# Folding W_self with W_c1 in the list stage of a two-layer graph kernel, with three orders of work changed beside it

## The chip, the cores and the metric

The kernel runs on one core of one Trainium2 chip. The metric is the device time of one execution in microseconds, as a median of runs. The core has five engines that run their own instruction streams in order: TensorE (PE, matmuls and their weight loads), VectorE (DVE), ScalarE (ACT), GpSimd (POOL) and SyncE (SP). SP issues most of the plain transfers, POOL issues the indirect ones, and ACT issues a few. They wait for each other by semaphores.

## The reference, cut to what matters

Two graph layers over 4096 nodes with 512 features, each with a residual and a layer norm. The adjacency matrix adj (4096 x 4096, int32) has about four ones in a row.

```python
# layer 0: graph attention, 8 heads of 64
Wh = einsum('nf,hfo->hno', x, W)
e  = leaky_relu(f1[:, :, None] + f2[:, None, :], 0.2)      # f1, f2 = Wh . a
attn = softmax(where(adj > 0, e, NEG_INF))
x = layernorm(x + concat_heads(attn @ Wh))
# layer 1: mean over neighbours
agg = (adj > 0) @ x / max(deg, 1)
out = concat([x @ W_self + b_self, agg @ W_nb + b_nb]) @ W_comb + b_comb
x = layernorm(x + relu(out))
```

With W_comb split into an upper half W_c1 and a lower half W_c2, layer 1 is x (W_self W_c1) + agg (W_nb W_c2) + one bias row, which is b_self W_c1 + b_nb W_c2 + b_comb. The kernel multiplies the weights first and calls that a fold.

## The kernel before, in words

Nodes are taken in 32 blocks of 128. All matmuls named here are float32 and fill 128 x 128 of the array. The order of the instructions on every engine is written out by hand: the program text is the order, and a tile name with its number of buffers says what may be reused when. PSUM tiles go by bank names: `tp` (1 buffer), `key` (1), `pw`, `nm` and `sm` (2 each).

**List stage.** It turns each row of adj into a short list of neighbours and computes Wh. The loop runs over b = 0 to 28. Step b loads adj of block b+2 in two halves of 1024 KB (tile `at`, 4 buffers, L389), loads a block of x, transposes x of block w+1 (`transposed`, L320, into `tp`, copied to `xT` by ACT), masks adj of block b+1 on ACT (L395, tile `ab`, 3 buffers), and calls `node_block`: half 0 of Wh (L341, into `pw`, copied by DVE to `row`, L345), the product that packs the masks of block b into keys (`fold_adj`, L413, into `key` or `nm`), the maxima of the keys on DVE (L428), half 1 of Wh, and the store of the row of Wh to the table t0 in HBM (L905, issued by POOL). In steps 6 and 13 two blocks of Wh are made. Every fourth step starts `decode`, which spreads the making of lists for four blocks over the next steps, mostly on DVE. In steps 22, 23 and 24 a further block is transposed only to be summed (`only=True`): DVE reduces it from PSUM (L330). Blocks 29 to 31 of adj follow the loop.

**Layer 1 of the schedule (reference layer 0)** is a loop over i = -2 to 32 with a pipeline over blocks. POOL gathers five groups of 128 rows of t0 for a block (`gather`, L590, 5 buffers of blocks). PE forms sums of weights (`a_shared_sum`, L638), spreads them back (`a_reach`, L657) and forms the shared products (`a_shared`, L684). DVE weighs and adds (L672, L694, L696) and forms the moments (L700); ACT normalises (L707 to L716). PE transposes the normalised block (L320) and multiplies it with the folded W_nb W_c2 (`a_z`, L721), and the row goes to the table t1. In steps 2 to 5 DVE adds b_nb's part to `brow` (`fold_bias`, L300); in step 7 SP loads W_self and W_c1; in steps 16 to 19 DVE adds b_self's part; in step 20 a matmul with ones sums `brow` over partitions (L308, copied by ACT, L309).

**Layer 2 (reference layer 1)** gathers five groups of rows of t1 for a block with 7 buffers of blocks, six late groups (`gather_late`, tile `gl`) among them. For a block PE forms the product with the folded W_self W_c1 (`g_self`, L753) and the shared products (`g_shared`, L760); ACT puts the bias row (L744) and the first gathered row (L734) in PSUM; DVE adds (L738, L740) and forms the output (L776, L780); ACT normalises; SP stores. Ahead of the first product with `m1`, `fold_weights` runs: for each of four chunks c, `turned` transposes 128 rows of W_self (L269, bank `key`, copied by ACT, L270), and four matmuls with W_c1 (L281, bank `tp`) give rows of the product, which ACT copies over `m1` (L285).

The lines of the loop of layer 1 that the change reorders:

```python
        if on(i):
            XT[i] = transposed(i, wp)
            store_xT(i, XT[i])
        if on(i + 2):
            a_shared_sum(i + 2)
        ...
        if on(i + 1):
            a_shared(i + 1)
```

Of the kernel before, what the change touches and what calls it, by code (L numbers as in the profile page):

```python
# [31 lines left out]
F32 = mybir.dt.float32  # L32
# [8 lines left out]
P = 128  # L41
# [49 lines left out]
def listed_layers(  # L91
# [15 lines left out]
    nc = tc.nc  # L107
    N, FIN = x.shape
    H, _, D = w0.shape
    NB = N // P  # L110
    FB = FIN // P
    HD = H * D
# [138 lines left out]
    def load_fold(k, w, wr, wc):  # L251
        nc.sync.dma_start(wr, w.rearrange("(c p) o -> p c o", p=P))
        nc.sync.dma_start(
            wc, w_comb[k * HD : (k + 1) * HD, :].rearrange("(c p) o -> p c o", p=P)
        )
        return wr, wc
# [6 lines left out]
            )  # L263
        return brw

    def turned(wr, c, wT):
        tp = ps.tile([P, FB, P], F32, name="key", bufs=1)
        for d in range(FB):
            nc.tensor.transpose(tp[:, d, :], wr[:, c, ts(d, P)], ident)  # L269
        nc.scalar.copy(wT, tp.rearrange("p c r -> p (c r)"))  # L270
        return wT.rearrange("p (c r) -> p c r", c=FB)

    def fold_weights(loaded, place):

        wr, wc = loaded
        wT = turned(wr, 0, place(0))
        for c in range(FB):
            nxt = turned(wr, c + 1, place(c + 1)) if c + 1 < FB else None
            mp = ps.tile([P, HD], F32, name="tp", bufs=1)
            for d in range(FB):  # L280
                nc.tensor.matmul(  # L281
                    mp, lhsT=wT[:, d, :], rhs=wc[:, d, :], start=(d == 0), stop=(d == FB - 1)
                )
                if d == FB - 1:
                    nc.scalar.copy(wr[:, c, :], mp)  # L285
                yield
            wT = nxt

    def bias_columns(brw):

# [6 lines left out]
    def fold_bias(loaded, bcol):  # L297

        for d in range(FB):
            nc.vector.scalar_tensor_tensor(  # L300
                brow, loaded[1][:, d, :], bcol[:, d : d + 1], brow, OP.mult, OP.add
            )
            yield
# [11 lines left out]

    def transposed(b, wp, sums=None, only=False):

        tp = ps.tile([P, FB, P], F32, name="tp", bufs=1)
        for c in range(FB):
            nc.tensor.transpose(tp[:, c, :], xs[:, b, ts(c, P)], ident)  # L320
        if only:
            t = tp
        else:
            t = wp.tile([P, FB, P], F32, name="xT", bufs=2)
        if sums is None or b >= EARLY and not only:
            nc.scalar.copy(t, tp)  # L326
        elif only or b % 2 == 0:
            if not only:
                nc.scalar.copy(t, tp)
            nc.vector.tensor_reduce(sums[:, :, b : b + 1], tp, AX.X, OP.add)  # L330
        else:
            for c in range(FB):
                nc.scalar.activation(
                    t[:, c, :], tp[:, c, :], AF.Copy, accum_out=sums[:, c, b : b + 1]
                )
        return t
# [56 lines left out]
    def mask_adj(b, h):  # L393
        ab = masks[b, h] = bp.tile([P, NG // NH, SC], BF16, name="ab", bufs=3)
        nc.scalar.activation(  # L395
            ab, loads.pop((b, h)), AF.Relu, accum_out=asum[:, b, h : h + 1]
        )
# [236 lines left out]
    def a_shared_sum(b):  # L634

        DN[b] = ps.tile([P, H], F32, name="sm", bufs=2)
        for k in range(KH):
            nc.tensor.matmul(  # L638
                DN[b], lhsT=OWN[b][:, k, :], rhs=E[b][:, K0 + k, :],
                start=(k == 0), stop=(k == KH - 1),  # L640
            )
# [40 lines left out]
    def a_shared(b):  # L682
        for k in range(KH):
            nc.tensor.matmul(  # L684
                NM[b], lhsT=OWN[b][:, k, :], rhs=G0[b][:, K0 + k, H:TW],
                start=False, stop=(k == KH - 1), skip_group_check=True,
            )

    def a_adds(b, wp):

        yp = ps.tile([P, HD], F32, name="pw", bufs=2)
        a_weigh(b, slice(0, 1), yp)
        a_weigh(b, slice(1, K0))
        nc.vector.tensor_add(yp, yp, G0[b][:, 1, H:TW])  # L694
        Y[b] = wp.tile([P, HD], F32, name="y", bufs=2)
        nc.vector.tensor_add(Y[b], yp, G0[b][:, 2, H:TW])  # L696
# [106 lines left out]
    def weight(pool, name):  # L803
        return pool.tile([P, FB, HD], F32, name=name)
# [75 lines left out]
    bcol = bias_columns(brw)  # L880


    def node_block(w, xT, between=None):
        row = wp.tile([P, FW], F32, name="row", bufs=2)
        node_half(w, 0, xT, w_sb, row)
        if between is not None:
            fold_adj(between, dp)
            max_keys(between)
        node_half(w, 1, xT, w_sb, row)
        node_rest(w, row)  # L890
        store(w, row, nc.gpsimd)
        return row

    def on_own(b):
# [9 lines left out]
    def store(w, row, eng=nc.scalar):  # L904
        eng.dma_start(t0[2 + w * P : 2 + (w + 1) * P, :], row[:, 0:TW])  # L905

    w, lists = 0, []
    for b in range(LB - 1):
        for k in range(1 + (b in AHEAD)):
            load_x(w + k + XL)  # L910
        load_adj(b + 2, ap)
        if b == 4:
            pads(wp)
        for k in range(2):
            some(lists)
        for k in range(1 + (b in AHEAD)):
            nxt = transposed(w + 1, wp, sums)
            if k == 0 and b in (22, 23, 24):
                transposed(EARLY + b - 22, wp, sums, True)
            if k == 0:  # L920
                key_bank(b + 1)
                for h in range(NH):
                    mask_adj(b + 1, h)
            node_block(w, xT, None if k else b)
            w, xT = w + 1, nxt
        for k in range(2):
            some(lists)
        if b == 16:
            lates = late_lists(dp, fp.tile([P, FB * HD // P, P], F32, name="wr"))
        if b >= 16:  # L930
            next(lates, None)
        if b == 25:
            pieces = mean_row(w_sb, sums, xa)
        if b >= 25:
            next(pieces, None)
        if b % G == G - 1:
            lists = [decode(b + 1 - G, dp, on_own)]
    load_adj(LB + 1, ap)
    node_block(w, xT)
    key_bank(LB)  # L940
    mask_adj(LB, 0)
    m2 = weight(fp, "wr")
    loaded = load_fold(1, w_nb, m2, weight(fc, "wc"))
    fold_adj(LB - 1, dp)
# [45 lines left out]
    def on(b):  # L990
        return 0 <= b < NB
# [3 lines left out]
    for i in range(-2, NB + 1):  # L995
        if on(i):
            a_moments(i)
        if on(i - 1 + GA):
            G0[i - 1 + GA] = gather(t0, i - 1 + GA, gps[(i - 1 + GA) % GA])
        elif i > 0:  # L1000
            b = i - 1 + GA - NB
            G1[b] = gather_early(b, gps[(NB + b) % GA])
        if on(i + 1):
            a_reach(i + 1)
        if i == -1:
            for k in range(2):
                next(m2s)
        if i >= -1 and on(i + 2):
            a_owned(i + 2, wq)
        if on(i + 1):  # L1010
            a_x(i + 1)
            a_normed(i + 1)
            a_weigh(i + 1, slice(K0, KS))
        if on(i + 2):
            a_weights(i + 2, wq)
        if on(i):
            root(i, xs[:, i, :])
        if on(i + 2):
            a_exp(i + 2)
        for k in range({-2: 3}.get(i, 0)):  # L1020
            some(lists)
        if on(i):
            norm(i, xs[:, i, :])
        if on(i - 1):
            a_z(i - 1, XT.pop(i - 1), m2, wp)
        if on(i + 1):
            a_adds(i + 1, wq)
        if on(i):
            XT[i] = transposed(i, wp)
            store_xT(i, XT[i])  # L1030
        if on(i + 2):
            a_shared_sum(i + 2)
            for k in range({-2: 1}.get(i, 0)):
                some(lists)
            a_sum(i + 2, wq)
            for k in range({-2: 1}.get(i, 0)):
                some(lists)
        for k in range({-2: 3, -1: 2}.get(i, 0)):
            next(m2s)
        if on(i + 1):  # L1040
            a_shared(i + 1)
        if on(i + 3):
            a_owners(i + 3, wp)
        if 2 <= i < 6:
            next(biased)
        if i == 7:
            loaded = load_fold(0, w_self, m1, weight(fc, "wc"))
        if 16 <= i < 20:
            if i == 16:
                biased = fold_bias(loaded, bcol[:, 0:FB])  # L1050
            next(biased)
        if i == 20:
            sum_bias()


# [15 lines left out]
    for b in range(2):  # L1071
# [2 lines left out]
        g_shared(b, G1[b])  # L1074
        g_adds(b, G1[b], wq)
        G1[b + GB] = gather(t1, b + GB, gps[b])
    for _ in fold_weights(loaded, place):
        pass
    for b in range(2):
        nxt = load_xT(b + 1, wp)  # L1080
        g_self(b, xT, m1)
# [447 lines left out]
```

## Time and profile before

| what | us |
|---|---|
| median of 3 runs (lowest, highest) | 692.57 (690.92, 694.48) |
| the profiled execution: its time | 690.14 |
| the profiled execution: its span | 688.4 |
| busy PE, DVE, ACT, POOL in the span | 622.5, 499.1, 456.0, 348.8 |
| last mask of adj on ACT starts | 229.18 |
| first gather of t0 starts | 232.54 |
| last product L721 of layer 1 starts | 483.35 |
| first shared product of layer 2 starts | 488.22 |
| last shared product of layer 2 ends | 677.1 |

All durations come from one profiled execution; its time is its span and 1.7 us around it. The list stage lasts to about 232 us, the start of layer 1 overlaps it to about 268, layer 1 lasts to 488 and layer 2 to the end. In the lines of a timeline the first number is the start in the span, the second the duration (of a whole group where instructions are merged, xN), and the bracket the idle time of the engine before it with what ended it. PE's busy time counts matmuls whose ends are modelled, so a busy PE isn't PE at its peak.

### The profile page before, as it was taken

What the parts mean: (1) busy time and instruction counts of PE and PEld (TensorE: products, weight loads), DVE (VectorE), ACT (ScalarE), POOL (GpSimd) and SP (SyncE); (2) the same over time, 40 slices, a digit from 0 to 9 for tenths busy, and PEclk for the clock granted to TensorE, in tenths of its full rate; (3) what the DMA queues carried; (4) which work ended last, traced back from release to release, by engine and by line L of the source; (5) the groups of instructions that cost most, each with busy time, mean ns of one, the idle gap of its engine ahead of it and who ended that gap; (6) DMA issues with size and microseconds to landing.
All of it is one profiled execution on the core that took longest, in us unless ns stands there. A gap on an engine that the chain in (4) does not pass through costs nothing.

```text
span 688.4 us, 9188 instructions
## 1 busy us (share of the span) xinstructions
PE 622.5 (90%) x2354; PEld 344.6 (50%) x2354; DVE 499.1 (72%) x1431; ACT 456.0 (66%) x1044; POOL 348.8 (51%) x411
## 2 busy tenths in 40 slices
PE   4798988987799597999999999999899999999993
PEld 2466766665567354545455445454344444444441
DVE  6237987998598787999998998897304666666663
ACT  3687988878487534767676767776316567767764
POOL 4011111110001477777677776746676677777760
PEclk9989999999899698999999999999999999999997
DMA  8999999999799877989989888868878899998992
GB/s 249 405 408 408 409 408 409 407 409 407 262 321 354 298 193 213 281 277 277 379 275 290 260 275 259 279 209 281 271 210 278 283 297 311 317 308 299 323 306 76
DMA packets 91974, 209.65 MB, mean 305 GB/s; under 512 B 13694, under 2 KB 13702, under 8 KB 91914
## 3 DMA queue, kind: packets, MB, share of 16 engines
q1 hardware_dynamic: 63024, 114.05, 44.8%
q0 software_dynamic: 28704, 94.66, 44.1%
q8 instruction: 21, 0.34, 0.2%
q14 instruction: 39, 0.32, 0.2%
q10 hardware_dynamic: 186, 0.28, 0.1%
HBM read 175.25 MB, written 33.69 MB: 304 GB/s over the span
## 4 chain that ended last, share of the span: by engine, by line
PE 56%; DVE 4%; DMA 4%; POOL 3%; issue 3%; ACT 2%; SPq 0%; DVEq 0%; POOLq 0%; ACTq 0%
PE pw L721 13%; PE nm L753 8%; PE pw L753 8%; PE nm L684 7%; PE nm L760 4%; PE pw L760 4%; POOL g L590 3%; PE tp L281 2%; PE tp L320 2%; PE pw L341 2%; PE sm L657 2%; DMA wc<-in_L_gnn_W_comb_dram 2%; PE sm L638 1%; DMA g<-t,idx 1%; DMA t<-row 1%
## 5 line engine op out<-in xcount | busy, mean ns | idle before, releaser
L590 POOL DMA_INDIRECT g<-t,idx x290 | 280.3, 967 | 109.1 <-issue 49.7
L395 ACT ACTIVATE ab<-at 128x2048 bf16<-128x2048 int32 x64 | 122.3, 1912 | 41.0 <-DMA at<-in_adj_dram 27.8
L341 PE MATMUL pw<-w_sb,xT 128*128 128x264 f32 x512 | 134.4, 409 | 7.0 <-issue 3.8
L721 PE MATMUL pw<-wr,xT 128*128 128x512 f32 x256 | 117.7, 603 | 0.7 <-ACT xT L326 0.7
L341 PEld LDWEIGHTS pw<-w_sb,xT 128*128 128x128 f32 x512 | 97.1, 199 | 36.0 <-issue 7.7
L352 POOL COPY f1s<-lst 128x24 f32<-128x24 f32 x32 | 7.8, 245 | 183.1 <-DVE fmax L349 100.5
L672 DVE TENSOR_TENSOR g<-g,key 128x1024 f32<-128x1024 f32 x64 | 77.9, 1217 | 1.1
L721 PEld LDWEIGHTS pw<-wr,xT 128*128 128x128 f32 x256 | 46.3, 191 | 47.2 <-issue 46.3
L684 PE MATMUL nm<-g,own 128*128 128x512 f32 x128 | 64.5, 627 | 0.0
L320 PE MATMUL tp<-ident,xs 128*128 128x128 f32 x268 | 44.9, 293 | 18.3 <-DVE sums L330 12.1
L753 PE MATMUL pw<-m,xT 128*128 128x512 f32 x128 | 57.6, 592 | 0.0
L753 PE MATMUL nm<-m,xT 128*128 128x512 f32 x128 | 57.6, 592 | 0.0
L320 PEld LDWEIGHTS tp<-ident,xs 128*128 128x128 f32 x268 | 32.3, 150 | 46.7 <-ACT xs L716 21.7
L707 ACT ACTIVATE xs<-y,ln_sum 128x512 f32<-128x512 f32 x32 | 23.1, 723 | 42.2 <-DVE y L700 40.2
L776 DVE SCALAR_TENSOR_TENSOR sm<-y,lst,nm 128x512 f32<-128x512 f32 x16 | 12.1, 756 | 52.9 <-PE nm L770 29.1
L345 DVE COPY row<-pw 128x264 f32<-128x264 f32 x64 | 26.9, 424 | 23.0 <-PE pw L341 17.4
L753 PEld LDWEIGHTS pw<-m,xT 128*128 128x128 f32 x128 | 24.4, 190 | 30.6 <-issue 30.3
L753 PEld LDWEIGHTS nm<-m,xT 128*128 128x128 f32 x128 | 24.4, 190 | 30.6 <-issue 30.6
L590 POOL DMA_INDIRECT g<-t,idxe x30 | 28.4, 947 | 18.2 <-issue 5.5
L281 PE MATMUL tp<-wc,row 128*128 128x512 f32 x64 | 30.9, 622 | 2.0 <-ACT m L285 1.2
L760 PE MATMUL nm<-g,own 128*128 128x512 f32 x64 | 30.2, 594 | 1.2 <-ACT nm L744 1.2
L684 PEld LDWEIGHTS nm<-g,own 128*128 128x128 f32 x128 | 22.5, 196 | 16.3 <-issue 15.6
(210 smaller groups left out, 1068.3 us busy)
## 6 DMA issues: line engine op xcount, KB each, us to landing
at<-in_adj_dram SPq DMA_DIRECT2D x64, 1024.0 KB, 10.7
t<-row POOLq DMA_DIRECT2D x32, 260.0 KB, 5.5
xt<-xT SPq DMA_DIRECT2D x32, 256.0 KB, 4.0
t<-row SPq DMA_DIRECT2D x32, 256.0 KB, 4.2
xT<-xt SPq DMA_DIRECT2D x32, 256.0 KB, 5.4
out_dram<-row SPq DMA_DIRECT2D x32, 256.0 KB, 5.2
xs<-in_x_dram SPq DMA_DIRECT2D x31, 256.0 KB, 10.9
g<-t,idx POOLq DMA_INDIRECT x290, 4.9
```

The lines of the kernel that those rows point to most:

```text
L281: nc.tensor.matmul(mp, lhsT=wT[:, d, :], rhs=wc[:, d, :], start=(d == 0), stop=(d == FB - 1))
L320: nc.tensor.transpose(tp[:, c, :], xs[:, b, ts(c, P)], ident)
L341: nc.tensor.matmul(pw, lhsT=xT[:, c, :], rhs=w_sb[:, c, k * HW : (k + 1) * HW], start=(c == 0), stop=(c == FB - 1),)
L345: nc.vector.tensor_copy(row[:, k * HW : (k + 1) * HW], pw)
L395: nc.scalar.activation(ab, loads.pop((b, h)), AF.Relu, accum_out=asum[:, b, h : h + 1])
L590: nc.gpsimd.indirect_dma_start(out=out, out_offset=None, in_=table, in_offset=bass.IndirectOffsetOnAxis(ap=at, axis=0),)
L672: nc.vector.tensor_tensor(gv if to is None else to.rearrange("p (k h d) -> p k h d", k=1, h=H), gv, E[b][:, sl].unsqueeze(3).to_broadcast( ...
L684: nc.tensor.matmul(NM[b], lhsT=OWN[b][:, k, :], rhs=G0[b][:, K0 + k, H:TW], start=False, stop=(k == KH - 1), skip_group_check=True,)
L707: nc.scalar.activation(wide, Y[b], AF.Square, bias=MV[b], scale=-float(HD), accum_out=rs)
L721: nc.tensor.matmul(pz, lhsT=xT[:, c, :], rhs=m2[:, c, :], start=(c == 0), stop=(c == FB - 1))
L753: nc.tensor.matmul(NM[b], lhsT=xT[:, c, :], rhs=m1[:, c, :], start=False, stop=(c == FB - 1), skip_group_check=True,)
L760: nc.tensor.matmul(NM[b], lhsT=OWN[b][:, k, :], rhs=g[:, K0 + k, 0:HD], start=False, stop=(k == KH - 1), skip_group_check=True,)
```

## The change

Four things. The early blocks of steps 22 to 24 are transposed into a `pw` bank instead of `tp`. The last row of Wh is stored by ACT's queue, after the first mask of block 30, and no longer by POOL's. In step i = 0 of layer 1, `a_shared_sum(2)` and `a_shared(1)` are issued ahead of the transposes of block 0. And the fold of W_self goes from the start of layer 2 to the list stage: the two loads in step 2, the four bias products in steps 4 to 7, the transposes of chunk c in step 7 + 2c (bank `pw`, copied to space in `xs` whose blocks 30 and 31 of x are loaded later), its four matmuls in step 8 + 2c (bank `nm`). Step 7 of layer 1 no longer loads weights, steps 16 to 19 no longer add a bias, and the matmul that sums `brow` goes from step 20 to step 6.

```diff
-    def turned(wr, c, wT):
-        tp = ps.tile([P, FB, P], F32, name="key", bufs=1)
+    def turned(wr, c, wT, bank=("key", 1)):
+        tp = ps.tile([P, FB, P], F32, name=bank[0], bufs=bank[1])
...
+    def fold_chunk(loaded, c, wT):
+
+        wr, wc = loaded
+        mp = ps.tile([P, HD], F32, name="nm", bufs=2)
+        for d in range(FB):
+            nc.tensor.matmul(
+                mp, lhsT=wT[:, d, :], rhs=wc[:, d, :], start=(d == 0), stop=(d == FB - 1)
+            )
+        nc.scalar.copy(wr[:, c, :], mp)
...
     def transposed(b, wp, sums=None, only=False):
 
-        tp = ps.tile([P, FB, P], F32, name="tp", bufs=1)
+        tp = ps.tile(
+            [P, FB, P], F32, name="pw" if only else "tp", bufs=2 if only else 1
+        )
...
-    def node_block(w, xT, between=None):
+    def node_block(w, xT, between=None, keep=False):
...
-        store(w, row, nc.gpsimd)
+        if not keep:
+            store(w, row, nc.gpsimd)
         return row
...
             node_block(w, xT, None if k else b)
             w, xT = w + 1, nxt
+        if b == 2:
+            loaded = load_fold(0, w_self, m1, weight(fc, "wc"))
+            biased = fold_bias(loaded, bcol[:, 0:FB])
+        if 4 <= b < 8:
+            next(biased)
+        if 7 <= b < 15 and b % 2:
+            wT = turned(m1, (b - 7) // 2, xs[:, NB - 2 + b // 2 % 2, :], ("pw", 2))
+        elif 7 <= b < 15:
+            fold_chunk(loaded, (b - 8) // 2, wT)
         for k in range(2):
             some(lists)
...
-    node_block(w, xT)
+    row = node_block(w, xT, keep=True)
     key_bank(LB)
     mask_adj(LB, 0)
+    store(w, row)
...
+        if i == 0:
+            a_shared_sum(i + 2)
+            a_shared(i + 1)
         if on(i):
             XT[i] = transposed(i, wp)
             store_xT(i, XT[i])
         if on(i + 2):
-            a_shared_sum(i + 2)
+            if i:
+                a_shared_sum(i + 2)
...
-        if on(i + 1):
+        if on(i + 1) and i:
             a_shared(i + 1)
...
-        if i == 7:
-            loaded = load_fold(0, w_self, m1, weight(fc, "wc"))
-        if 16 <= i < 20:
-            if i == 16:
-                biased = fold_bias(loaded, bcol[:, 0:FB])
-            next(biased)
-        if i == 20:
+        if i == 6:
             sum_bias()
...
-    for _ in fold_weights(loaded, place):
-        pass
     for b in range(2):
         nxt = load_xT(b + 1, wp)
         g_self(b, xT, m1)
```

## The prediction

> **What bounds the kernel now.** I read the page's slices and its chain that ended last, then the windows and the timeline of each stretch that the diff touches.
>
> ```profile
> PE   4798988987799597999999999999899999999993
> GB/s 249 405 408 408 409 408 409 407 409 407 262 321 354 298 193 213 281 277 277 379 275 290 260 275 259 279 209 281 271 210 278 283 297 311 317 308 299 323 306 76
> ...
> PE 56%; DVE 4%; DMA 4%; POOL 3%; issue 3%; ACT 2%; SPq 0%; DVEq 0%; POOLq 0%; ACTq 0%
> ```
>
> A slice is 17.2 us. In slices 2 to 10 the transfers stand near 408 GB/s: there the list stage waits for adj. The 56% on PE are layers 1 and 2. The windows (busy us of PE, weight load, DVE, ACT, POOL; clock, DMA share, GB/s) show that PE in the list stage is nearly full too:
>
> ```profile
> 60.00:115.00 55.00, 50.45 (x293) 37.25 (x292) 44.30 (x177) 45.84 (x95) 7.46 (x20) 1.00 1.05 408
> 115.00:172.00 57.00, 49.39 (x287) 36.33 (x287) 51.67 (x213) 47.59 (x95) 6.81 (x18) 0.97 1.05 408
> 172.00:190.00 18.00, 12.65 (x70) 9.18 (x69) 9.78 (x33) 8.73 (x16) 1.49 (x4) 0.81 0.73 256
> ```
>
> The third window holds a stall. Its timeline lines (start, us, engine, line, operation; in brackets the idle time before and its releaser):
>
> ```profile
> 179.29 0.68 DVE L330 TENSOR_REDUCE sums<-tp 128x4 f32<-128x512 f32 x1
> 180.03 1.11 PE L320 MATMUL tp<-ident,xs 128*128 128x128 f32 x4 [4.80 <-DVE sums L330]
> 180.94 3.72 PE L341 MATMUL pw<-w_sb,xT 128*128 128x264 f32 x8
> ```
>
> The early block's transposes wait 4.80 us for the single tp bank, which VectorE reads late, and then PE runs at half speed (3.72 us where others take 1.95). Layer 1 begins with a similar stall, layer 2 with the fold of W_self, and layer 2 ends close behind the gathers:
>
> ```profile
> 268.05 1.12 PE L320 MATMUL tp<-ident,xs 128*128 128x128 f32 x4 [3.41 <-ACT xs L716]
> 273.47 0.69 DVE L700 SCALAR_TENSOR_TENSOR y<-y,nm 128x512 f32<-128x512 f32 x1 [2.67 <-PE nm L684]
> 491.76 0.60 PE L269 MATMUL key<-ident,m 128*128 128x128 f32 x4
> 506.55 3.70 PE L281 MATMUL tp<-wc,row 128*128 128x512 f32 x8 [0.68 <-ACT m L285]
> 545.35 0.95 POOL L590 DMA_INDIRECT g<-t,idx  x1 [1.68 <-DVE sm L738]
> 668.38 0.95 POOL L590 DMA_INDIRECT g<-t,idx  x1 [0.30 <-issue]
> 678.35 0.76 DVE L776 SCALAR_TENSOR_TENSOR sm<-y,lst,pw 128x512 f32<-128x512 f32 x1
> ```
>
> From 545.35 to 668.38 lie 98 gathers, 1.255 us each, without a wait: POOL is full while PE is full.
>
> [...] the stalls of 4.80 and 3.41 us are followed by half-speed matmuls[...].[...] here POOL's share of a 260 KB store is 0.55 us.[...] all 326 gathers here are POOL's[...].
>
> **1. The fold leaves layer 2: -6.8 us.** PE loses 16 transposes (0.60 to 0.66 us per four), 16 matmuls of 128x512 (3.70 us per four) and waits, from 491.3 to 509.7: 18.4 us. ACT loses eight copies of 0.585 us that lay beside them. Late next is POOL: its 26 gather groups from G1[6] on start at 503.07, right behind layer 1's stores and the six late gathers, which do not move. Before 545 POOL waited 3.4 us in all beyond its 0.30 us issue gaps, for buffers that block 2 and the next ones release; these waits go, as PE reaches block 2 near 515 and G1[9] is wanted at 522. So the last gather starts at 503.07 + 129 x 1.255 = 665.0 (668.38 before). The reading of its rows now follows at once: 5.5 us to landing (median of the last 40 us), 0.9 us for the last shared product, 0.2 us, so L776 of block 31 near 671.6 instead of 678.35: -6.8. Bounds: -3.4 (only the waits) and -9.0 (landing in 3.3 us, the shortest gather).
>
> **2. The fold enters the list stage: +13.8 us.** Two loads of 1024 KB stand on SP behind adj of block 4, ahead of x and adj of the next steps: 2.10 MB at 408 GB/s are 5.1 us while everything waits for adj. The bias step at b=4 wants wc near 49 us; issued near 36 with 13.0 us to landing it is just there; up to 2 us if not. Four bias products of 0.70 us go to DVE at b=4 to 7, beside the wait for adj: nothing, up to 2.8 without that cover. On PE, steps 7 to 14 gain 4 x 0.66 + 4 x 3.43 = 16.4 us. ACT's copy of a chunk waits up to 3.4 us for PE; behind it stand the xT copy, the key copy and the next two masks, hence the release of two adj buffers and SP's next loads. Those masks are wanted only one step later, and four adj buffers (2.6 us each) let DMA run 10 us ahead: nothing, up to 3 us if DMA stops. PE's bracketed waits from 63 to 172 us sum to 12.1: 4.5 in steps 7 to 14, of which I take 4.0 as filled; 2.5 for masks, which are then early; 1.2 that part 3 removes; 3.8 for DVE, which stay. So 5.1 + 16.4 - 7.7 = +13.8; with all waits filled +9.4, with only the 4.0 filled +17.5.
>
> **3. Early transposes in a pw bank: -7.6 us.** At b=22, 23, 24 they no longer wait for tp. At b=22 (its 1.23 us counted above) the half-speed cost of 1.35 goes. At b=23 4.80 + 0.45 + 1.77 us go, but the second half product then needs that pw bank, free only when DVE has summed it, near 179.1 on the old scale: 2.2 us of new wait, so -4.8. At b=24 -1.5. After 172 us DMA has room (256 GB/s), so PE's gain counts. Bounds: -9.8, and -1.6 if DVE, 51.67 of 57 us busy, keeps the pace.
>
> List stage together: +6.2, from -0.4 (9.4 - 9.8) to +15.9 (17.5 - 1.6).
>
> **4. Last row from ACT: +0.3 us.** POOL loses a 0.55 us issue. ACT issues after the mask of block 30, waits for the row (224.69), then for its own issue, about 0.3 us; the next mask, which began at 224.85, is behind it, and PE's folds wait for that mask (1.9 us shown). No 260 KB store from ACT is in the trace; its 256 KB load took 4.0 us against 5.5 for POOL's stores, so the first gather starts 0 to 3 us sooner than 232.54. That hides behind the last decode, DVE's from 232 to 258. Bounds +0.5 and -0.5.
>
> **5. First step: -2.0 us.** At i=0 the sums of block 2 and the shared products of block 1 run ahead of the transposes, which wait for the norm. They can start when exp is ready, 267.3, after 2.65 us idle instead of 3.41. If the clock holds, the shared products end at 269.8 instead of 273.4 and DVE's L700 moves 2.7, PE's next product 2.1. If it falls, 0.7. I take 2.0. Late next is DVE's sum for block 2.
>
> **6. Layer 1: -0.8 us.** The four bias products of steps 16 to 19 go: these steps took 7.08 us where neighbours take 6.87. The column sum moves from step 20 to step 6 at equal cost. The two loads of step 7 left no wait in the trace: nothing.
>
> **Sum.** 6.2 + 0.3 - 2.0 - 0.8 - 6.8 = -3.1 us. On the profiled execution (span 688.4, time 690.14) that is 687.0; it stands 2.4 us under the median 692.57, so I forecast 689.5.
>
> **Rivals.**
> - *Everything fills up*: PE's idle time takes the fold, list stage -0.4: sum -9.7, 682.9. For it: PE's record counts overlapping ends as busy. Against: PE and DVE are coupled through one tp and two pw banks.
> - *The list stage pays, slower*: PE is the bound from step 7 on, and DVE keeps the early-block stalls: list stage +15.9, sum +6.6, 699.2. For it: both windows above show PE at 87 to 92% and DVE at 81 to 91%. It decides from a list stage longer by 13 us (9.3 gained elsewhere and the 3.5 that a measurement tells).
> - *The whole fold is won in layer 2*: 18.4 instead of 6.8, 677.9. Against it stand the 98 gathers without a wait.
> - *The change does not do what it says*: the code issues the fold at steps 7 to 14 and nowhere else, so hardly.
>
> **How the numbers follow.** The forecast 62%, the list stage pays 20%, everything fills 15%, whole fold 3%. Half a per cent, 3.5 us, is about what a measurement of this kernel can tell from no change. The forecast lies at that edge: 0.28 faster, 0.32 same, 0.02 slower of its 0.62. With the rivals: faster 0.46, same 0.32, slower 0.22. The forecast's own range is 685 to 694; with most of both rivals, 681 to 699.
>
> **What would show it.** Adj's last mask (229.18 before) near 235; no long tp wait near b=23; the chunk products (3.4 us) in steps 8, 10, 12, 14 and PE's waits there gone; L700 of block 1 without its 2.67 us; PE idle before shared products late in layer 2, with the chain there on POOL gathers; and layer 2, from its first shared product (488.22) to the end of the span, 6.8 us shorter than 200.2. I am wrong if PE stays full to the end of layer 2, or if the last mask comes after 242 or before 229.

## The result and the profile after

The changed kernel takes 698.36 us (median of 20 runs, 693.76 to 700.12), the kernel before 692.85 us in the same sitting (20 runs). The ratio is 1.0062, 95% interval 1.0045 to 1.0080: **slower by 4.3 us**, 3.1 to 5.5 (the two medians lie 5.5 us apart, the two means 4.6). On another chip it was 1.0065 (1.0045 to 1.0085). The forecast was 3.1 us faster.

The profiled execution has a span of 696.5 us and a time of 698.23, at its median; that of before, at 690.14, was 2.7 us under its median here. So the two profiles differ by 8.1 us where the medians differ by less. Of the page, the busy tenths of PE and the GB/s in 40 slices of 17.4 us:

```profile
PE   4787999988889779899999999999889999999982
GB/s 246 408 406 409 408 396 382 352 343 408 358 243 360 345 247 202 209 257 250 277 252 296 278 277 282 266 248 251 269 276 306 288 303 319 314 304 318 307 292 86
```

Slices 6 to 9, 87 to 157 us, no longer carry 408 GB/s. There stand the four products of the fold, and the transfers wait for PE (the kernel `loads_only` below, which leaves the products out, shows 408 again). The windows say it in busy us (span of the window, then PE, weight load, VectorE, ScalarE, POOL with their counts; granted clock, DMA share, GB/s):

```profile
60.00:115.00 55.00, 53.74 (x294) 38.52 (x289) 41.39 (x155) 45.79 (x88) 7.31 (x16) 0.97 1.03 396
115.00:172.00 57.00, 53.64 (x303) 38.58 (x301) 46.53 (x186) 45.71 (x96) 6.81 (x18) 1.00 0.99 371
172.00:190.00 18.00, 14.01 (x80) 10.26 (x80) 15.15 (x68) 11.77 (x22) 1.60 (x5) 0.91 1.01 375
```

PE rose from 87 to 92% to 94 to 98% of the first two windows. The stall at b=23 is still there, now ahead of the second half product. From the timeline of PE and VectorE (start, us, engine, line, operation, tiles; in brackets the idle time before and what ended it):

```profile
193.77 0.68 DVE L342 TENSOR_REDUCE sums<-tp 128x4 f32<-128x512 f32 x1
194.37 0.68 DVE L342 TENSOR_REDUCE sums<-pw 128x4 f32<-128x512 f32 x1
...
195.10 2.62 PE L353 MATMUL pw<-w_sb,xT 128*128 128x264 f32 x8 [2.63 <-DVE sums L342]
197.52 3.45 PE L505 MATMUL sm<-lst,own 128*128 128x24 f32 x16
```

The first product of the fold, in step 8, reads so in the same timeline:

```profile
85.84 3.60 PE L294 MATMUL nm<-wc,xs 128*128 128x512 f32 x8
```

At b=23 PE no longer waits for tp. It waits for the pw bank that the early transposes have taken, and VectorE reads that bank 0.6 us after it reads tp, behind the same decode. PE then runs at half speed: the lists' products take 3.45 us, which took 1.86 in before.

At the end of layer 2 the idle time is PE's, as forecast. The pieces of the chain that ended last (start, us, what):

```profile
676.27 0.95 POOL g L602
677.22 0.30 issue
677.53 4.92 DMA g<-t,idx
682.44 0.14 issue
682.58 3.77 PE pw L772 x4
```

A gather, its landing, then the last shared product, which runs cold: 3.77 us against 1.88, at a granted clock of 0.50, after 3.50 us in which PE had idled.

Span of each stretch, taken from starts in the timelines. The second column is the profile above, the third the same kernel profiled again.

| stretch, us | before | after | after, again |
|---|---|---|---|
| start to adj's last mask | 229.18 | 243.00 | 239.71 |
| to layer 1's first norm (Square of block 0) | 35.95 | 39.26 | 36.21 |
| to the Square of block 3 | 22.76 | 21.77 | 24.54 |
| to layer 2's first shared product | 200.33 | 198.74 | 198.78 |
| to the end of the span | 200.18 | 193.73 | 192.86 |
| span | 688.4 | 696.5 | 692.1 |

The list stage costs more than layers 1 and 2 give back. But two profiles of one kernel differ by about 3 us in three of the five stretches, so no term below is read from one profile alone where others are at hand. **Markers** in what follows: "b=22" is the start of that step's first transposes (166.56 in before), "b=25" likewise (195.49). One reading of the kernel before has to be put right for what follows: not all products named there are float32 on 128 x 128; those of `fold_adj` are bf16 on 128 x 32.

### The profile page after: what moved, and what is told of

The parts are those of the page before. It is cut to its first block, busy times and chain, and to the rows that moved or that the text cites. A ratio compares the mean times of both kernels' runs of the same rounds, so it can differ in the third digit from the quotient of the medians.

```text
span 696.5 us, 9189 instructions
## 1 busy us (share of the span) xinstructions
PE 629.4 (90%) x2354; PEld 348.4 (50%) x2354; DVE 499.6 (72%) x1431; ACT 455.0 (65%) x1044; POOL 347.2 (50%) x410
## 5 line engine op out<-in xcount | busy, mean ns | idle before, releaser
L353 PE MATMUL pw<-w_sb,xT 128*128 128x264 f32 x512 | 136.1, 413 | 10.0 <-issue 3.8
L407 ACT ACTIVATE ab<-at 128x2048 bf16<-128x2048 int32 x64 | 122.2, 1916 | 27.4 <-DMA at<-in_adj_dram 22.8
L733 PE MATMUL pw<-wr,xT 128*128 128x512 f32 x256 | 117.7, 602 | 1.0 <-ACT xT L338 1.0
L364 POOL COPY f1s<-lst 128x24 f32<-128x24 f32 x32 | 9.3, 290 | 195.3 <-DVE lst L360 100.6
L733 PEld LDWEIGHTS pw<-wr,xT 128*128 128x128 f32 x256 | 46.3, 190 | 47.7 <-issue 46.4
L765 PE MATMUL nm<-m,xT 128*128 128x512 f32 x128 | 59.3, 608 | 2.9 <-DMA xT<-xt 2.9
L719 ACT ACTIVATE xs<-y,ln_sum 128x512 f32<-128x512 f32 x32 | 23.1, 723 | 38.2 <-DVE y L712 38.2
L332 PEld LDWEIGHTS tp<-ident,xs 128*128 128x128 f32 x256 | 30.7, 147 | 34.2 <-ACT xs L728 17.1
L332 PE MATMUL tp<-ident,xs 128*128 128x128 f32 x256 | 41.3, 286 | 6.3 <-DVE sums L342 6.0
L788 DVE SCALAR_TENSOR_TENSOR sm<-y,lst,nm 128x512 f32<-128x512 f32 x16 | 12.1, 755 | 41.6 <-PE nm L772 25.6
L772 PE MATMUL pw<-g,own 128*128 128x512 f32 x64 | 32.1, 626 | 4.1 <-DMA g<-t,idx 4.1
L788 DVE SCALAR_TENSOR_TENSOR sm<-y,lst,pw 128x512 f32<-128x512 f32 x16 | 12.1, 755 | 29.4 <-PE pw L772 26.6
```

The lines of the kernel that those rows point to most:

```text
L353: nc.tensor.matmul(pw, lhsT=xT[:, c, :], rhs=w_sb[:, c, k * HW : (k + 1) * HW], start=(c == 0), stop=(c == FB - 1),)
L407: nc.scalar.activation(ab, loads.pop((b, h)), AF.Relu, accum_out=asum[:, b, h : h + 1])
L719: nc.scalar.activation(wide, Y[b], AF.Square, bias=MV[b], scale=-float(HD), accum_out=rs)
L733: nc.tensor.matmul(pz, lhsT=xT[:, c, :], rhs=m2[:, c, :], start=(c == 0), stop=(c == FB - 1))
L765: nc.tensor.matmul(NM[b], lhsT=xT[:, c, :], rhs=m1[:, c, :], start=False, stop=(c == FB - 1), skip_group_check=True,)
L772: nc.tensor.matmul(NM[b], lhsT=OWN[b][:, k, :], rhs=g[:, K0 + k, 0:HD], start=False, stop=(k == KH - 1), skip_group_check=True,)
```

## Experiments

Totals are ratios to the kernel before on the same chip, five rounds each.

**One part at a time.** The four kernels are before with one part of the diff each. First the fold (the whole of the change but the early transposes, the last row and the first step):

> The fold and its bias are moved to the list stage, the other three parts undone. Theory A (the steps around the fold are full of PE work, each added us of PE or DMA costs a us): adj's last mask 15 us after 229.18, near 244; layer 2 6.5 us shorter than 200.2; total 6.5 to 9 us over before, ratio near 1.011. Theory B (the fold itself is as cheap as the prediction had it, +13.8, and the other parts spoil it): last mask near 243, total 6.2 us over before, and then the changed kernel is no better than this one. Theory C (the fold is cheap, as PE and DMA hide it): last mask before 239, total within 2 us of before.

Measured: 700.22 us (8 runs), ratio 1.0074 (1.0045 to 1.0103). Last mask 242.75, b=22 at 181.45, layer 2 194.37 us. Nearer theory B than A: the last mask is where B has it, the total, 5.1 us over before by the ratio, is near what the prediction's own terms give (+6.2), and the fold alone is as slow as the whole change. C falls.

> Only the early blocks' transposes go into a pw bank; the fold stays in layer 2. Prediction: list stage 7.6 us shorter, last mask near 221.6, total 7.6 us under before (ratio 0.989). Theory A (VectorE's order of work holds the bank just as it held tp, and PE still goes cold): the second half product of b=23 waits 2.6 us for the sums, last mask 1.7 us earlier, 227.5, total 1 to 2 us under before. Theory B (in the changed kernel the fold had spoiled this part; alone it brings what was predicted): last mask before 224.

```
-        tp = ps.tile([P, FB, P], F32, name="tp", bufs=1)
+        tp = ps.tile(
+            [P, FB, P], F32, name="pw" if only else "tp", bufs=2 if only else 1
+        )
```

Measured: 690.92 us, ratio 0.9947 (0.9929 to 0.9965), **3.7 us faster**; last mask 226.54. Theory A has the mechanism right and the size too low: it had 1 to 2 us. Its timeline of PE in steps 22 to 24:

```profile
168.25 3.35 PE L343 MATMUL pw<-w_sb,xT 128*128 128x264 f32 x8 [0.46 <-DVE row L347]
...
180.33 2.05 PE L343 MATMUL pw<-w_sb,xT 128*128 128x264 f32 x8 [2.64 <-DVE sums L332]
...
189.34 3.67 PE L343 MATMUL pw<-w_sb,xT 128*128 128x264 f32 x8 [2.03 <-DVE sums L332]
```

Step 23 is 4.6 us shorter (9.62 against 14.22 us from its transposes to the next), close to the 4.8 forecast. Step 24 is 2.3 us longer (8.94 against 6.67): its early block sits in a pw bank as well, and VectorE reaches it only behind the decode's last piece. In before the same product had no wait:

```profile
193.60 2.05 PE L341 MATMUL pw<-w_sb,xT 128*128 128x264 f32 x8
```

The forecast had 1.5 us of gain there. At b=22 the half speed stays: 3.35 us for the first half product, where others take 1.95.

> Only the order of layer 1's first step is changed. Prediction: 2.0 us under before. Theory A (PE still idles 2.7 us ahead of the shared products and then runs at half speed): 0.6 to 1.0 us under before, shared products of block 1 at about 3.5 us. Rival: the transposes, now behind cold shared products, come 3 us later and the first product with M2 with them, total 0 to 1 us over before.

```
+        if i == 0:
+            a_shared_sum(i + 2)
+            a_shared(i + 1)
         if on(i):
             XT[i] = transposed(i, wp)
...
```

Measured: 694.63 us, ratio 1.0012 (0.9992 to 1.0032). No gain is measured; the rival's 0 to 1 us fits, theory A's 0.6 to 1.0 us of gain lies at or past the end of the interval. PE in the first step of this kernel:

```profile
269.52 1.02 PE L638 MATMUL sm<-e,own 128*128 128x8 f32 x4 [2.72 <-ACT e L632]
270.40 3.76 PE L684 MATMUL nm<-g,own 128*128 128x512 f32 x4
273.95 1.06 PE L320 MATMUL tp<-ident,xs 128*128 128x128 f32 x4
```

The idle time is 2.72 us instead of 3.41, and PE goes cold all the same: the shared products take 3.76 us, as in before, where they take 1.88 at full speed. The cold shared products now stand ahead of the transposes and of M2's first product.

> Only the last row is stored from ScalarE. Prediction: +0.3 us (bounds -0.5 to +0.5), last mask 0.3 us later than 229.18. Rival: it is this part that made the stretch from the last mask to layer 1's first norm 3.3 us longer in the changed kernel; then that stretch, 35.95 us in before (229.18 to 265.13), is near 39 here, total +3.5 us. Without that, the stretch stays 36.

Measured: 694.34 us, ratio 1.0001 (0.9982 to 1.0019); last mask 228.39; ScalarE's store of 260 KB landed in 6.2 us. The part costs nothing that this measurement can tell. The stretch to layer 1 was 38.40 us, as the rival had it. But first_only, which changes nothing ahead of that norm, had 38.49, so the rival is not shown.

**What in the list stage costs.**

> The changed kernel with the two loads and the bias of the fold in the list stage, but its transposes and products made nowhere (W_self itself stands in the place of the product). It separates the price of the loads from that of PE. The prediction's terms: loads 5.1 us, products 16.4 less filled waits. Theory A (terms add): last mask 3 to 5 us after 229.18 less the 0.4 to 2.6 that the early transposes save, so 231 to 234; total 7 to 10 us under the changed kernel, that is 3 to 5 us under before. Theory B (the loads are hidden, all of the +13.8 is PE's): last mask at 227 to 229. Theory C (the loads are the price, as DMA bounds the stage to 172 us and PE only follows): last mask after 240.

```
-        if 7 <= b < 15 and b % 2:
-            wT = turned(m1, (b - 7) // 2, xs[:, NB - 2 + b // 2 % 2, :], ("pw", 2))
-        elif 7 <= b < 15:
-            fold_chunk(loaded, (b - 8) // 2, wT)
```

This kernel leaves the product out, so it prices work and is no version to use. Measured: 685.4 us (6 runs), ratio 0.9869 (0.9823 to 0.9915), last mask 230.25. Nearest to theory A, though neither number is in its range: the mask is 0.75 us early, and the total is 9.1 us under before (5.9 to 12.3) where A had 3 to 5. It has b=22 at 171.41, that is 4.85 us after before's; the changed kernel has it at 181.61. So of the 15.05 us, **the loads, with their bias products, are 4.85 and PE's transposes and products 10.2** (10.6 against the changed kernel's second profile). The windows of this kernel show what the products take away:

```profile
60.00:115.00 55.00, 51.20 (x296) 37.75 (x291) 46.59 (x182) 46.76 (x94) 8.12 (x18) 0.97 1.05 408
115.00:172.00 57.00, 51.10 (x294) 37.11 (x293) 49.50 (x200) 46.83 (x89) 6.82 (x18) 0.97 1.05 408
```

Without products the transfers are back at 408 GB/s. With them they move 396 and 371 GB/s, and PE, busy for 98 and 94% of the two windows, is the bound.

> The changed kernel with one chunk of the fold per three steps (steps 7 to 18) instead of two (7 to 14). Theory A (a 3.4 us product every second step is more than the lead of the four adj buffers and PE's idle time per step can take, so DMA stops; thinner, PE's waits of 0.6 us a step and the lead absorb more of it): last mask 2 to 5 us ahead of the changed kernel's 243.0, total 2 to 5 us under it. Theory B (PE has next to no idle time that is not needed, each added us of PE costs one): last mask 242 to 244, total within 1.5 us of the changed kernel (ratio to before 1.005 to 1.008).

```
-        if 7 <= b < 15 and b % 2:
+        if 7 <= b < 19 and (b - 7) % 3 == 0:
...
-        elif 7 <= b < 15:
+        elif 7 <= b < 19 and (b - 7) % 3 == 1:
```

(with `// 3` in the chunk's number). Measured: 696.20 us, ratio 1.0035 (1.0016 to 1.0054), last mask 241.0. The total is at the edge of A. But b=22 stands at 181.00, 0.6 us ahead of the changed kernel, which is B; the rest came later, from b=22 to 25 (24.51 us against 27.23), where the two kernels do the same work and the clock differs (6.83 us of half clock against 13.65). Against the changed kernel's second profile (last mask 239.71) nothing of it is left. The spacing of the products matters little.

> The fold in the list stage once more, on the kernel early_act_only, but its four products stand where PE was seen to wait: ahead of the transposes of b=22 (2.2 us), between the two half products of b=23 and 24 (2.4 and 0.6 us), and after the last node block (1.9 us); its loads are issued at b=14, transposes at b=18 and 20, the bias at b=25 to 28. Theory A (what a product costs depends on whether PE would have waited there; in steps 7 to 14 the 16.4 us of PE cost 12.75): last mask 5 to 9 us after early_act_only's 227.59, so 232 to 237, layer 2 near 194, total 0 to 4 us under early_act_only (ratio to before 0.988 to 0.993). Theory B (PE and VectorE are coupled so closely that work put into a wait only moves the wait): last mask 239 to 244, total 4 to 8 us over early_act_only (ratio 0.999 to 1.005).

```
...
+        if b == 22:
+            fold_chunk(loaded, 0)
         for k in range(1 + (b in AHEAD)):
             nxt = transposed(w + 1, wp, sums)
...
             max_keys(between)
+            if between in (23, 24):
+                fold_chunk(loaded, between - 22, ("nm", "sm")[between % 2])
         node_half(w, 1, xT, w_sb, row)
...
     mask_adj(LB, 0)
+    fold_chunk(loaded, 3)
...
```

This kernel doesn't compute the reference's values, for a reason that isn't shown here, so it too prices work and is no version to use. Measured on a chip on which the kernel before took 807.3 us: 799.53, ratio 0.9979 (0.9945 to 1.0012), last mask 240.61. The last mask is theory B's, the total neither's. From b=22 to b=25, with two products of 3.7 us inside, it took 24.26 us, and early_act_only without them 25.81. That doesn't show that a product in a wait is free: the granted clock was full all through these steps here and half for 10.24 us of them in early_act_only. And b=22 came 12.9 us later (loads, transposes and the first product ahead of it), and the fourth product held a mask:

```profile
235.69 0.58 ACT L298 COPY m<-nm 128x512 f32<-128x512 f32 x1 [3.99 <-PE nm L295]
236.28 1.91 ACT L407 ACTIVATE ab<-at 128x2048 bf16<-128x2048 int32 x1
```

ScalarE waits 3.99 us to copy the product, and the next mask is behind that copy in its order.

**What holds PE at b=23.**

> Kernel before, with the early blocks' transposes in a pw bank as in the changed kernel, but their column sums taken on ScalarE (four activations with an accumulated sum, some 0.45 us each) instead of VectorE. Theory A (what is left of the stall is VectorE's reading of the pw bank, behind the decode): the waits of 2.64 and 2.03 us ahead of the second half products of b=23 and 24 go, PE keeps its clock, the last mask comes 4 to 6 us ahead of early_only's 226.54, near 221.6, which is what the prediction counted for this part; total 7 to 9 us under before (ratio 0.988). Rival B (ScalarE is late too, or tp is still held by VectorE, and PE waits there instead): last mask within 1.5 us of 226.5, total as early_only, 0.9947. Rival C (the sums delay the masks behind them by 2 us each in three steps): last mask later than 228.

```
...
-        elif only or b % 2 == 0:
-            if not only:
-                nc.scalar.copy(t, tp)
+        elif b % 2 == 0 and not only:
+            nc.scalar.copy(t, tp)
```

Measured: 689.55 us, ratio 0.9933 (0.9913 to 0.9953), last mask 227.59. Rival B: the second half products no longer wait for sums, and another of VectorE's readers takes their place at b=23.

```profile
179.30 2.60 PE L342 MATMUL pw<-w_sb,xT 128*128 128x264 f32 x8 [2.37 <-DVE row L346]
181.69 3.45 PE L494 MATMUL sm<-lst,own 128*128 128x24 f32 x16
```

With the early transposes in one pw bank and the first half product in the other, the second half product needs one of them back. VectorE has yet to copy the row, behind the decode.

> early_act_only, with VectorE's work reordered: every fourth step (b=23 among them) no longer starts with two pieces of the decode, these go to the step's end, and the last two pieces to the start of the next step. It asks whether VectorE's order is what holds PE at b=23. Theory A: the wait of 2.37 us ahead of the second half product of b=23 goes, PE keeps its clock there, last mask 2 to 4 us ahead of early_act_only's 227.59, total 1.5 to 4 us under it (ratio to before 0.988 to 0.991). Theory B (VectorE has no room, what is put off is waited for later): a wait of like size stands at b=24, last mask within 1.5 us of 227.59, total as early_act_only (0.9933).

```
...
-        for k in range(2):
+        for k in range(2 if b % G < G - 1 else 0):
             some(lists)
...
-            lists = [decode(b + 1 - G, dp, on_own)]
+            lists = lists[-1:] + [decode(b + 1 - G, dp, on_own)]
```

Measured on the same chip as holes: 802.74 us against 807.3, ratio 0.9906 (0.9852 to 0.9959), too wide to tell. So it was run again:

> The kernel pieces once more, as its first run was on a chip where the kernel before took 807 us, with slower gathers. Theory A (VectorE's order held PE at b=23): ratio to before 0.988 to 0.991, 1.5 to 4 us under early_act_only's 0.9933, last mask near 226. Theory B (what is put off is waited for later): 0.992 to 0.995.

Measured: 690.14 us, ratio 0.9958 (0.9937 to 0.9979), last mask 224.42. The wait at b=23 falls from 2.37 to 0.55 us, as A says:

```profile
178.35 2.05 PE L342 MATMUL pw<-w_sb,xT 128*128 128x264 f32 x8 [0.55 <-DVE row L346]
```

The last mask comes 3.2 us ahead of early_act_only's, earlier than A had it. But the total gains nothing on early_act_only (0.9933), and is a little above B's range. In the profiles the stretch from the last mask to layer 1's first norm is 38.54 us against 36.23, which takes back 2.3 us; in it the clock falls a second time, as is told below. VectorE's order holds PE at b=23, and mending that one place does not shorten the kernel measurably.

**Is the early part worth less beside the fold?**

> The changed kernel as it is, beside fold_only on one chip, for what the early transposes are worth once the fold is in the list stage. Theory A (with the fold there, steps 22 to 25 had already lost most of their stall, so the early transposes bring almost nothing): within 1.5 us of fold_only, ratio to before 1.005 to 1.008, last mask 242.5 to 243.5. Theory B (they bring the same 3.7 us as alone): 3 to 4 us under fold_only, ratio 1.002 to 1.004. And for the stretch from the last mask to layer 1's first norm, 39.26 us in the first profile of the changed kernel and 35.7 to 36.2 in others: if it is a matter of when the clock falls, it may be 36 here with nothing changed.

> fold_only as it was, beside the changed kernel on one chip. Theory A: ratio to before 1.006 to 1.010, last mask 242.5 to 243.5, the stall at b=23 with its wait of 4.80 us for tp still there, steps 22 to 25 (from the transposes of b=22 to those of b=25) 27.6 us against 28.9 in before. Theory B: ratio 1.006 to 1.010 too, and the changed kernel 3 to 4 us under it.

Measured on one chip: 1.0065 (1.0045 to 1.0085) and 1.0097 (1.0065 to 1.0130), medians 698.09 and 700.07. The difference, 2.2 us with an interval of about 2.6 either way, leaves both theories open; it is in neither's range, though the changed kernel's ratio is in A's. It is also the sum of three parts: with the first step at +0.8 and the last row at +0.1 us, as measured alone, the early part beside the fold would be an estimated 3.1 us. The stall of 4.80 us is there in fold_only_again, but its last mask came at 245.3 and from b=22 to b=25 it took 29.70 us and not 27.6, so theory A's numbers are missed as well. The changed kernel's own second profile has 23.35 us for these steps where the first had 27.23:

```profile
183.55 2.02 PE L353 MATMUL pw<-w_sb,xT 128*128 128x264 f32 x8 [0.46 <-DVE row L357]
...
194.45 2.05 PE L353 MATMUL pw<-w_sb,xT 128*128 128x264 f32 x8 [2.63 <-DVE sums L342]
196.34 1.86 PE L505 MATMUL sm<-lst,own 128*128 128x24 f32 x16
...
203.46 2.05 PE L353 MATMUL pw<-w_sb,xT 128*128 128x264 f32 x8 [2.02 <-DVE sums L342]
```

The same wait of 2.63 us as in the first profile, and the clock holds: the lists' products take 1.86 us, not 3.45. And the stretch from the last mask to layer 1 is 36.21 us where the first had 39.26, with no change in the program: a matter of when the clock falls.

**A version that beats both kernels** is before with the early transposes in a pw bank alone: 0.9947, or 0.9933 with their sums on ScalarE (these two intervals overlap). The fold stays in layer 2.

## Why the prediction was wrong, by its steps

Each term by the runs that carry or lack it. For "22 to 25" the kernels without the early part had 28.93, 27.83, 27.84, 27.59 and 29.70 us (before, first_only, last_only, fold_only twice), those with it as the change has it 26.16, 27.23, 23.35, 23.34 and 24.51 (early_only, changed twice, loads_only, spread3): means 28.4 and 24.9.

| term | predicted | measured | from |
|---|---|---|---|
| 1 fold leaves layer 2 | -6.8 | -6.9 | six profiles with 192.9 to 194.4 us, six without 200.2 to 200.8 |
| 2 fold enters the list stage | +13.8 | +14.8 to +15.4 | b=22 in changed and fold_only, twice each |
| 3 early transposes | -7.6 | -3.5 to -3.7 | 22 to 25; early_only's total |
| 4 last row | +0.3 | +0.1, within 1.3 | last_only's total |
| 5 first step | -2.0 | +0.8, -0.6 to +2.2 | first_only's total |
| 6 layer 1 | -0.8 | -1.5 | Square of block 3 to layer 2: 198.7 to 198.9 (six) against 200.2 to 200.3 (four) |
| sum | -3.1 | about +4 | changed kernel: +4.3 |

Left out of row 6 are early_only, with 204.9, and last_only, with 201.7 us: each is held up at one place in layer 1, early_only by a wait of PE of 2.79 us at 342.99. The two profiles from the chip with 807 us stand in no row.

**Term 1 held**, and by its own steps. From the first gather of G1[6] to the last it took 516.94 to 678.78 in the changed kernel, 161.84 us for 129 intervals (161.9 forecast), with no wait. Of the second half, 3.4 us from reading the rows at once, 2.4 came (678.78 to VectorE's L788 at 686.37, against 9.97 us before): the last shared product, for which the working had 0.9 us, takes 1.88 at full speed and ran cold, in 3.77. Another 0.7 us came before the first gather.

**Term 2 held.** Its 13.8 us count 1.2 us of waiting that stands behind the mark b=22; up to the mark it comes to 15.0, against 14.8 to 15.4. Loads 4.85 (5.1 forecast), PE 16.4 less 6.2 of filled waits (6.5 forecast, without those given to term 3). The products in steps 8, 10, 12 and 14 take 3.60 us, and in steps 7 to 14 PE waits nowhere longer than 0.9 us. With term 3 at half its size, the list stage as a whole became 13.8 and 10.5 us longer in the two profiles, about the 13 us from which the rival "The list stage pays, slower" decides. That rival's total, 699.2 us, is near the measured one, and its reason is the right one in part: PE is the bound and VectorE keeps the stalls. But its +15.9 us for the list stage wasn't reached, and layer 1's first step, which it counted as a gain, brought none.

**Term 3 is the step that failed**, by 4 us (5.3 in steps 22 to 25, with the 1.2 us of waiting there that term 2 had counted). The step at b=23 is right: 4.8 forecast, 4.6 measured. "At b=24 -1.5" was wrong in sign: +2.3 in early_only, and +0.6 in the two profiles in which the clock held from b=22 to b=25 (7.30 us against 6.67). The working asked who holds the pw bank at b=23 and counted VectorE's sums there (2.2 us, measured 2.63), but not at b=24, where the same question gives 2.0 us of new wait. "At b=22 the half-speed cost of 1.35 goes" was wrong too, in those executions where the clock falls. The lower bound in the text, -1.6 "if DVE keeps the pace", is about what the first profile shows (27.23 against 28.93 us); the value taken stood nearer the other end.

**Term 5 failed** as well, by some 3 us. The prediction named the case (0.7 "if it falls") and took 2.0 "if the clock holds". It fell, and then more was lost than the working allowed. In kernels without this edit the Squares of blocks 0 and 3 lie 22.8 to 23.1 us apart (seven profiles, without those from the chip with 807 us). With it they lie 21.8, 22.7, 24.5, 24.5 and 24.6: in the long ones M2's first product (L733 in the changed kernel) takes about 5.7 us instead of 3.70. In the changed kernel's second profile:

```profile
279.01 3.76 PE L696 MATMUL nm<-g,own 128*128 128x512 f32 x4
282.57 1.06 PE L332 MATMUL tp<-ident,xs 128*128 128x128 f32 x4
...
284.30 5.68 PE L733 MATMUL pw<-wr,xT 128*128 128x512 f32 x8
```

**Term 6** was mis-sized: steps 16 to 19 without their bias products take 6.72 us on average, where the working took 6.87 from one neighbour.

**The clock sorts these profiles.** The record of the granted clock in each trace tells how much of a stretch ran at half clock:

| stretch | half clock, us | length, us |
|---|---|---|
| b=22 to 25, early blocks in tp | 6.83; 10.24 | 27.6 to 27.8 (three); 28.9, 29.7 |
| the same, early blocks in pw | 0; 3.41; 6.83; 13.65 | 23.3, 23.4; 24.5; 26.2; 27.2 |
| Square of block 0 to 3, first step changed | 3.41; 6.83; 10.24 | 21.8; 22.7; 24.5 to 24.6 (three) |

At equal half clock, 6.83 us, the early part brings 1.4 to 1.7 us and the first step 0.1 to 0.4. The rest of the 3.5 us of term 3 came with less half clock; whether the edit keeps the clock up, or these five profiles had luck, they can't tell.

**The signs that were set beforehand.** The last mask came at 243.0 and 239.7 where near 235 was forecast: once past the bound of 242 that was to count as wrong, once short of it. The long wait for tp near b=23 went. L712 of block 1 waits 0.58 and 1.22 us in the two profiles instead of 2.67; the stretch around it became 1.0 us shorter in the one and 1.8 us longer in the other. PE idles before the late shared products. Layer 2 is 6.45 and 7.3 us shorter.

**What stays open.** The early part's worth beside the fold, with the last row and the first step, is known only as 2.2 us, give or take 2.6. The stretch to layer 1 is 38.4 to 39.3 us in seven profiles and 35.7 to 36.2 in five. In each of the seven the record has a second stretch of half clock, of 3.4 or 6.8 us, between the last mask and the norm, and in none of the five. Whether that is more frequent in one kernel than in another can't be told from one or two profiles each.

## What to carry to other kernels

Moving a tile to another buffer to be rid of a wait only helps if that buffer's reader is earlier (at b=23 a wait of 4.80 us became one of 2.6, at b=24 one of 2.0 us came where none had been): ask it at every place where the move acts, not at the worst one. Here the work moved out of a stage where POOL was nearly as full as PE brought little over a third of its length (6.9 of 18.4 us), and moved into a stage where PE was 90% busy it cost nearly two thirds (10.2 of 16.4), plus its loads (4.85 us). Before a part is put into a sum of several, price the parts alone: here one of them, alone, was the faster kernel.

## What the runs showed of the hardware

The half-speed stretches of PE decide gains of this size. The length of a wait alone didn't tell whether one follows: with the same instructions and the same wait of 2.63 us the clock fell in one execution of the changed kernel and not in the next, and the steps from b=22 to b=25 took 27.23 and 23.35 us. It fell after idle times of 2.63 and 2.70 us in the first of them and of 2.72 us in first_only, so cutting the gap in layer 1's first step from 3.41 to 2.7 us did not save the clock.

The traces show what goes with it. In each of them the stretches between two changes of the clock last 3.41 us or a whole multiple of it (6.83, 10.24, 13.65). With each trace cut into windows of 3.41 us on this grid, PE's idle time by the records was 2.0 us or more in 101 of the windows at full clock in the fourteen traces (6 of them in before, 7 in the changed kernel's first profile), and all 101 were followed by half clock. Of the 2419 with less than 1.75 us only 17 were (none in before, one in the changed kernel's first profile, from 264.71 us with 0.40 us idle), and in all 17 the lists' products of 19 or 24 columns are what PE did most. Of the changed kernel's two waits of 2.63 us, the first profile's had 2.08 us in one window (193.03 to 196.44), and the clock fell; the second's was split, with at most 1.71 us in one, and it held. So in these traces a wait's share in one window told more than its length, and this program doesn't control that share; and with products as thin as these the clock fell while PE's record was busy.

On one chip the kernel before took 807.3 us and on the others 692.7 to 694.1. There the list stage was as elsewhere (last mask 226.24 and 224.42 in the two runs of pieces) and the stages of gathers were longer: from the Square of block 3 to layer 2 232.6 instead of 200.2 us, layer 2 251.4 instead of 200.8; POOL once waited 15.27 us for ScalarE between two gathers, the cause of which was not followed up.
